# Local attention of a two-layer decoder: the rotation's second product in its own buffer, ahead of the sum of squares, and the sum's lower bound from a column in SBUF

## The chip, the core and the metric

The kernel runs on one core of a Trainium2 chip. A core has TensorE (PE in the profile, with its weight loads as PEld), VectorE (DVE), ScalarE (ACT), GpSimd (POOL) and SyncE (SP), which issues transfers. Each engine takes its instructions in the order of the program and waits on semaphores for the others. The metric is the device time of one execution in microseconds (us). It is the median of the runs.

## The reference, cut to what matters

The model is a decoder of two layers on x of 4 x 512 x 128. The change lies in the last block, a local attention with its feed-forward part, which has two layers of its own and runs over 4 x 512 tokens in each.

```
def l2norm(t):
    return t / jnp.clip(jnp.linalg.norm(t, axis=-1, keepdims=True), 1e-12)
def rotate_half(x):
    x1, x2 = jnp.split(x, 2, axis=-1)
    return jnp.concatenate([-x2, x1], axis=-1)
...
    h = shift_token(x)
    q, k, v = jnp.split(h @ wqkv, 3, axis=-1)      # 8 heads of 64
    q = l2norm(q) * qs
    k = l2norm(k) * ksc
    q = q * cos * scale + rotate_half(q) * sin * scale
    k = k * cos / scale + rotate_half(k) * sin / scale
    o = local_attention(q, k, v)                   # windows of 64, with the one before
    x = x + o @ wo
    h = layernorm(shift_token(x)) @ w1 + b1
    a, g = jnp.split(h, 2, axis=-1)
    x = x + (a * gelu(g)) @ w2 + b2
```

The norm's lower bound of 1e-12 becomes a bound of 1e-24 on the sum of squares.

## The kernel before, in words

The tokens are cut into 16 tiles of 128 (four for each of the four sequences). Two layers make 32 tiles, numbered `i` from 0 to 31. In the local attention nothing is scheduled by a planner: the order of every engine's queue is the order of the calls, written out by hand.

The main loop goes over `g`, two steps for each tile (`p` is 0 or 1, four of the eight heads each). A step calls `scores(g + 1)`, then `others(g, 0)`, `weights(g)`, `others(g, 1)`, `exponentials(g + 1)`, `values(g - 1)` and `others(g, 2)`. `others` takes its calls from the table `around` (L1805) with a distance in tiles: the projections of a tile start three tiles ahead of its attention. For tile `i + 3`:

- step p=0, slot 2: `project_qk` writes q and k of the tile into the PSUM buffer `pqk` (there is one), and `squares` (ScalarE) squares it into the SBUF buffer `sq` (there is one).
- step p=1, slot 0: `rotated_a` (VectorE) multiplies `pqk` by the cosine table into `ta`.
- step p=1, slot 1: `norms` (VectorE) sums `sq` over 64 into `ss` of 128x16 and bounds it from below (L1466, L1467). `rotated_b` follows: `halves` (VectorE, two instructions, L1480) multiplies the swapped halves of `pqk` by the sine table into `tb`. `halves_added` (POOL) adds `tb` to `ta`, `lengths` (POOL) raises `ss` to the power -0.5 into `rn`, and `scaled` (POOL) multiplies `ta` by `rn`.
- two tiles later `turn_k` and `turn_q` (PE) transpose the result into the PSUM buffers `ptk` and `ptq`.

`tb` has the tag `sq` with one buffer, so the square and the second product of a tile share one place in SBUF. `pqk` comes free when `sq`, `ta` and `tb` have been computed from it. It also serves the feed-forward part: `ff_gates`, in the step p=1, slot 2 of every fourth tile, puts its first two products `pff2` there.

PSUM tiles of the tag `pt` rotate over three buffers: `pv`, `po`, `ptp`, `ptk`, `ptq` and the feed-forward products take them in turn. A buffer comes free when it has been read: that of `po` by `xa` on VectorE (L1589), the residual sum in `output`, which stands behind `rotated_b` in the same step.

VectorE's order in the step with p=1 is: `nm` (the maximum of the scores, L1540), `ta`, `ss`, the bound, `tb`, then `rc` and `at` of `values` (L1570, L1571), then `xa`, then `nm` of the next step. In one step of every four tiles `ge` (L1641, a feed-forward product) stands between `tb` and `rc`.

Ahead of the main loop stands the cross attention, whose steps carry the first three tiles of the local attention in a list of their own, `first`. It calls `norms`, `rotated_a`, `halves`, `halves_added`, `lengths` and `scaled` one by one.

Of the kernel before, what the change touches and what calls it, by code (L numbers as in the profile page):

```python
# [11 lines left out]
F32 = mybir.dt.float32  # L12
# [3 lines left out]
ALU = mybir.AluOpType  # L16
# [3 lines left out]
P = 128  # L20
# [37 lines left out]
def decoder_kernel(ctx: ExitStack, tc: tile.TileContext, a: dict):  # L58
    nc = tc.nc
    V, S, G, TE = nc.vector, nc.scalar, nc.gpsimd, nc.tensor  # L60


    cp = ctx.enter_context(tc.tile_pool(name="const", bufs=1))
# [44 lines left out]
    G.memset(cminus, -1.0)  # L108
    eps = cp.tile([P, 1], F32, tag="eps", name="eps")
    G.memset(eps, 1e-5)  # L110


    hm16 = cp.tile([P, 16], F32, tag="hm16", name="hm16")
# [123 lines left out]
    with ExitStack() as ph:  # L237
# [176 lines left out]
        with tc.tile_pool(name="m2", bufs=3) as t2, \  # L414
# [159 lines left out]
            with tc.manual_schedule():  # L574
# [7 lines left out]
                for k in range(n_):  # L582
# [19 lines left out]
                    if aside and (n in (9, 10, 13, 14) or b == B - 1 and n < 11):  # L602
                        f, of = aside.pop(0)
# [815 lines left out]
    with tc.tile_pool(name="la_b", bufs=2) as bp, tc.tile_pool(name="la_t", bufs=2) as t1, \  # L1419
# [14 lines left out]
        hTs, pqks, tas, tbs, rns, sss, qTs, pes, pTs, ats, aTs = ({} for _ in range(11))  # L1434
# [28 lines left out]
        def norms(i):  # L1463

            ss = sm.tile([P, 16], F32, tag="ss16", name="ss16")
            V.tensor_reduce(ss, sss.pop(i).rearrange("p w h d -> p (w h) d"), AX.X, ALU.add)  # L1466
            V.tensor_scalar_max(ss, ss, 1e-24)  # L1467
            sss[i] = ss

        def rotated_a(i):  # L1470
# [3 lines left out]

        def halves(i):
            src = pqks.pop(i).rearrange("p w (h d) -> p w h d", d=64)
            tb = tbs[i] = t1.tile([P, 2, 8, 64], F32, tag="sq", name="tb", bufs=1)
            for hf in range(2):
                lo = slice(32 * hf, 32 * hf + 32)
                V.tensor_tensor(  # L1480
                    tb[:, :, :, lo], src[:, :, :, 32 - 32 * hf:64 - 32 * hf],
                    tabs[i // NT][:, i % NJ, 1, :, lo].unsqueeze(2).to_broadcast([P, 2, 8, 32]), ALU.mult)
# [11 lines left out]
            G.tensor_tensor(ta, ta, rns.pop(i).unsqueeze(2).to_broadcast([P, 16, 64]), ALU.mult)  # L1494

        def rotated_b(i):
            for f in (halves, halves_added, lengths, scaled):
                f(i)

        def turn_q(i):  # L1500
# [291 lines left out]
        def x_norm(b):  # L1792
            normal(x5[:, b * NJ:(b + 1) * NJ, :], *mvs.pop(("x", b)))


        first = {9: [(shift, 0)], 10: [(project_qk, 0), (squares, 0)],
                 11: [(norms, 0), (rotated_a, 0), (halves, 0), (halves_added, 0)],
                 12: [(project_qk, 1), (squares, 1), (lengths, 0)],
                 13: [(project_v, 0), (norms, 1), (rotated_a, 1), (halves, 1), (scaled, 0)],
                 14: [(halves_added, 1), (project_qk, 2), (squares, 2)], 15: [(lengths, 1), (turn_k, 0), (turn_q, 0)],  # L1800
                 16: [(project_v, 1), (norms, 2), (rotated_a, 2), (halves, 2), (scaled, 1)],
                 17: [(halves_added, 2)], 18: [(lengths, 2), (scores, 0)], 19: [(scaled, 2), (exponentials, 0)]}


        around = [[[], [(turn_k, 1), (turn_q, 1)], [(project_qk, 3), (squares, 3)]],  # L1805
                  [[(turn_out, -1), (rotated_a, 3)], [(norms, 3), (rotated_b, 3)], [(project_v, 2), (output, -1)]]]

        feed = {(0, 0): [[], [], [(ff_hidden, 2, 0)]], (0, 1): [[], [(ff_hidden, 2, 1)], []],
                (1, 0): [[(ff_shift, 1)], [(ff_hidden, 2, 2)], []],
# [14 lines left out]
        with tc.manual_schedule():  # L1824
# [25 lines left out]
            for g in range(last):  # L1850
                i, p = divmod(g, 2)
# [183 lines left out]
```

## Time and profile before

| | us |
|---|---|
| median of three runs | 1233.97 (1232.23 to 1235.54) |
| the profiled execution | 1233.73, its span 1231.7 |
| PE busy | 1081.4 (88%) |
| VectorE busy | 895.8 (73%) |
| ScalarE busy | 731.2 (59%) |
| POOL busy | 644.7 (52%) |
| `ss`, 32 sums | 38.7, 1209 ns each |
| the bound, 32 | 6.5, 202 ns each (174 in the median) |
| `tb`, 64 halves | 40.9, 681 ns each |
| POOL `ta<-ta,tb`, 32 | 75.4, 2356 ns each |
| POOL `rn`, 32 | 93.0, 2906 ns each |
| POOL `ta<-ta,rn`, 32 | 60.8, 1901 ns each |

The span is the time from the first to the last instruction on the core. Busy times of the engines overlap, and matmuls are pipelined, so a busy PE isn't a PE at its peak. In the rows, L1466 is line 1466 of the kernel; `out<-in` are the names of the tiles. The local attention's loop fills the trace from about 842 us to 1180 us, and the granted TensorE clock there is 1.00.

### The profile page before, as it was taken

What the parts mean: (1) busy time and instruction counts of PE and PEld (TensorE: products, weight loads), DVE (VectorE), ACT (ScalarE), POOL (GpSimd) and SP (SyncE); (2) the same over time, 40 slices, a digit from 0 to 9 for tenths busy, and PEclk for the clock granted to TensorE, in tenths of its full rate; (3) what the DMA queues carried; (4) which work ended last, traced back from release to release, by engine and by line L of the source; (5) the groups of instructions that cost most, each with busy time, mean ns of one, the idle gap of its engine ahead of it and who ended that gap; (6) DMA issues with size and microseconds to landing.
All of it is one profiled execution on the core that took longest, in us unless ns stands there. A gap on an engine that the chain in (4) does not pass through costs nothing.

```text
span 1231.7 us, 22149 instructions
## 1 busy us (share of the span) xinstructions
PE 1081.4 (88%) x8377; PEld 698.5 (57%) x8377; DVE 895.8 (73%) x1691; ACT 731.2 (59%) x1629; POOL 644.7 (52%) x554
## 2 busy tenths in 40 slices
PE   5879879787778889989999998787999999999995
PEld 2324333443456679966666665455666566666564
DVE  5878888898668274867867676787777676676753
ACT  5696867764364454546566665246665765766762
POOL 5458586776454432644201111367786576576641
PEclk9799989898799899999999999899999999999998
DMA  9000000000400342300000000000110110011100
GB/s 280 1 0 1 0 1 1 0 1 0 154 1 14 137 154 76 85 27 25 2 2 2 2 2 2 0 9 19 32 28 18 28 27 18 22 24 28 27 20 28
DMA packets 38739, 39.96 MB, mean 32 GB/s; under 512 B 7544, under 2 KB 29833, under 8 KB 38153
## 3 DMA queue, kind: packets, MB, share of 16 engines
q1 hardware_dynamic: 36041, 32.73, 9.2%
q0 software_dynamic: 2048, 4.20, 1.2%
q10 hardware_dynamic: 544, 1.62, 0.5%
q8 instruction: 66, 1.08, 0.4%
q14 instruction: 40, 0.33, 0.1%
HBM read 20.80 MB, written 9.18 MB: 24 GB/s over the span
## 4 chain that ended last, share of the span: by engine, by line
PE 46%; DVE 18%; ACT 4%; issue 2%; POOL 2%; DMA 1%; DVEq 0%; ACTq 0%; POOLq 0%; SPq 0%
PE psc L189 9%; PE pa L189 4%; PE pqk L189 4%; PE ptp L1287 4%; PE po L189 3%; PE pff L189 3%; PE phg L189 3%; PE pog L189 3%; DVE tb L1480 2%; PE pv L189 2%; DVE ss L1466 2%; DVE ta L1473 2%; PE pof L189 2%; PE pq L189 1%; DMA hn<-xa 1%
## 5 line engine op out<-in xcount | busy, mean ns | idle before, releaser
L451 POOL TENSOR_TENSOR h<-h,cb 128x1024 f32<-128x1024 f32 (+1 forms) x65 | 151.8, 2337 | 72.0 <-DVE h L446 59.8
L157 POOL TENSOR_TENSOR rs<-ve,cneg 128x1 f32<-128x1 f32 (+2 forms) x74 | 56.1, 758 | 210.9 <-DVE ve L166 175.7
L446 DVE TENSOR_TENSOR_SCAN h<-dA,pb 128x1024 f32<-128x1024 f32 x64 | 146.3, 2286 | 21.7 <-PE y L189 7.4
L1277 ACT ACTIVATE pe<-psc,nm 128x256 f32<-128x256 f32 (+1 forms) x256 | 93.4, 448 | 69.7 <-DVE nm L1270 68.9
L189 PE MATMUL y<-h,ident 128*128 128x512 f32 x256 | 128.9, 628 | 6.1 <-POOL h L451 5.4
L1486 POOL TENSOR_TENSOR ta<-ta,tb 128x1024 f32<-128x1024 f32 x32 | 75.4, 2356 | 102.5 <-DVE rc L1570 56.2
L1270 DVE TENSOR_REDUCE nm<-psc 128x4 f32<-128x1024 f32 (+1 forms) x64 | 69.8, 1090 | 43.1 <-PE psc L189 37.9
L157 POOL TENSOR_TENSOR rn<-ss,cneg 128x16 f32<-128x16 f32 x32 | 93.0, 2906 | 0.0
L1540 DVE TENSOR_REDUCE nm<-psc 128x4 f32<-128x512 f32 x64 | 44.0, 687 | 63.8 <-PE psc L189 62.0
L438 ACT ACTIVATE dA<-delta,negA 128x511 f32<-128x511 f32 (+1 forms) x128 | 85.3, 715 | 6.3 <-POOL delta L352 4.4
L189 PEld LDWEIGHTS y<-h,ident 128*128 128x128 f32 x256 | 49.7, 198 | 67.5 <-issue 47.2
L940 ACT ACTIVATE hTg<-phg,bias 128x128 f32<-128x128 f32 x184 | 52.3, 368 | 46.6 <-PE phg L189 45.0
L443 DVE TENSOR_TENSOR pb<-du,pb 128x1024 f32<-128x1024 f32 x64 | 77.5, 1211 | 2.4 <-POOL du L355 1.5
L1549 ACT ACTIVATE pe<-psc,nm 128x128 f32<-128x128 f32 x256 | 73.6, 380 | 5.0 <-DVE nm L1540 4.9
L189 PE MATMUL pqk<-f_qkv,hT 128*128 128x512 f32 x128 | 65.0, 631 | 4.1 <-DVE tb L1480 4.1
L1287 PE MATMUL ptp<-ident,pe 128*128 128x128 f32 x448 | 64.9, 282 | 4.0 <-ACT pT L1289 2.0
L189 PE MATMUL psc<-kb,qk 64*128 64x256 f32 (+1 forms) x512 | 66.4, 378 | 0.0
L189 PE MATMUL pb<-stk,sel 96*128 96x512 bf16 x128 | 41.2, 405 | 25.9 <-DVE h L446 15.5
L1494 POOL TENSOR_TENSOR ta<-ta,rn 128x1024 f32<-128x1024 f32 x32 | 60.8, 1901 | 2.4
L1287 PEld LDWEIGHTS ptp<-ident,pe 128*128 128x128 f32 x448 | 48.7, 141 | 20.4 <-ACT pT L1289 7.8
L1460 ACT ACTIVATE sq<-pqk 128x1024 f32<-128x1024 f32 x32 | 32.9, 1029 | 43.6 <-PE pqk L189 40.3
L189 PE MATMUL pff<-hnT,f_w 128*128 128x512 f32 (+3 forms) x108 | 48.7, 571 | 9.6 <-DVE tb L1480 7.3
(391 smaller groups left out, 2810.1 us busy)
## 6 DMA issues: line engine op xcount, KB each, us to landing
vh<-va SPq DMA_DIRECT2D x56, 130.0 KB
w<-in_e_w_dram SPq DMA_DIRECT2D x16, 256.0 KB
xs<-zero SPq DMA_DIRECT2D x2, 1472.0 KB
xg<-xs SPq DMA_DIRECT2D x10, 256.0 KB
ys<-yg SPq DMA_DIRECT2D x10, 256.0 KB
f_qkv<-in_f_qkv_dram SPq DMA_DIRECT2D x1, 1536.0 KB
x<-in_x_dram SPq DMA_DIRECT2D x4, 256.0 KB
w_kv<-in_w_kv_dram SPq DMA_DIRECT2D x1, 1024.0 KB
```

Source lines behind the costliest of these rows:

```text
L157: G.tensor_tensor(out, in_, cneg.to_broadcast([P, n]), ALU.pow)
L189: TE.matmul(out, lhsT=lhsT, rhs=rhs, start=start, stop=stop)
L438: S.activation(dAs[k % 4][:, c, c:T], delta[b % 2][:, c, c:T], AF.Exp, scale=negA[:, c * NST + n:c * NST + n + 1])
L443: V.tensor_tensor(pb, du[steps[k][0] % 2], pb, ALU.mult)
L446: V.tensor_tensor_scan(h.rearrange("p c t -> p (c t)"), dAs[k % 4].rearrange("p c t -> p (c t)"), pb.rearrange("p c t -> p (c t)"), 0.0, A ...
L451: G.tensor_tensor(h[:, c], h[:, c], cb.unsqueeze(1).to_broadcast([P, n, T]), ALU.mult)
L1270: V.tensor_reduce(nm, psc[:, :, 0:nk], AX.X, ALU.max, negate=True)
L1277: S.activation(pe[:, h, 0:nk], psc[:, h, 0:nk], AF.Exp, bias=nm[:, h:h + 1])
L1287: TE.transpose(ptp[:, h * nb + kk, :], pe[:, 2 * pr + h, kk * P:(kk + 1) * P], ident)
L1486: G.tensor_tensor(ta, ta, tbs.pop(i).rearrange("p w h d -> p (w h) d"), ALU.add)
L1494: G.tensor_tensor(ta, ta, rns.pop(i).unsqueeze(2).to_broadcast([P, 16, 64]), ALU.mult)
L1549: S.activation(pes[g][:, h, :], o[:, par, q, :], AF.Exp, bias=nm[:, k:k + 1])
```

## The change

Three edits. The product `tb` gets its own buffer, tag `tb`. In the main loop `norms` moves into `rotated_b`, behind `halves` and `halves_added` and ahead of `lengths`; in the lead-in list `first` the order stays. The bound is no longer a `tensor_scalar` with a number, but a `tensor_tensor` whose second input is a column `least` of SBUF, spread over 16 elements; POOL fills the column once at the start.

```diff
     eps = cp.tile([P, 1], F32, tag="eps", name="eps")
     G.memset(eps, 1e-5)
+    least = cp.tile([P, 1], F32, tag="least", name="least")
+    G.memset(least, 1e-24)
...
             V.tensor_reduce(ss, sss.pop(i).rearrange("p w h d -> p (w h) d"), AX.X, ALU.add)
-            V.tensor_scalar_max(ss, ss, 1e-24)
+            V.tensor_tensor(ss, ss, least.to_broadcast([P, 16]), ALU.max)
             sss[i] = ss
...
-            tb = tbs[i] = t1.tile([P, 2, 8, 64], F32, tag="sq", name="tb", bufs=1)
+            tb = tbs[i] = t1.tile([P, 2, 8, 64], F32, tag="tb", name="tb", bufs=1)
...
         def rotated_b(i):
-            for f in (halves, halves_added, lengths, scaled):
+            for f in (halves, halves_added, norms, lengths, scaled):
                 f(i)
...
-                  [[(turn_out, -1), (rotated_a, 3)], [(norms, 3), (rotated_b, 3)], [(project_v, 2), (output, -1)]]]
+                  [[(turn_out, -1), (rotated_a, 3)], [(rotated_b, 3)], [(project_v, 2), (output, -1)]]]
```

With it VectorE's order in the step with p=1 is `nm`, `ta`, `tb`, `ss`, the bound, `rc`, `at`, `xa`. POOL's order is the same as before, apart from the one `memset`. ScalarE's squares no longer wait for POOL; the queues of PE, ScalarE and SP keep their order.

## The prediction

> **What bounds the kernel now.** I began with the chain of work that ended last on the page.
>
> ```profile
> PE 46%; DVE 18%; ACT 4%; issue 2%; POOL 2%; DMA 1%; DVEq 0%; ACTq 0%; POOLq 0%; SPq 0%
> PE psc L189 9%; PE pa L189 4%; PE pqk L189 4%; PE ptp L1287 4%; PE po L189 3%; PE pff L189 3%; PE phg L189 3%; PE pog L189 3%; DVE tb L1480 2%; PE pv L189 2%; DVE ss L1466 2%; DVE ta L1473 2%; PE pof L189 2%; PE pq L189 1%; DMA hn<-xa 1%
> ```
>
> PE carries the chain, but three VectorE groups of the change's own stage stand in it: `tb`, `ss` and `ta`. That stage, the local attention, runs from 842 to 1180 us in the trace. The windows view has PE busy 45.6 of every 47.37 us there (a period of four token tiles), so it looks like a PE stage. The question is what releases PE. I read VectorE through one plain step in the timeline, then PE and POOL at the same place (columns: start us, us, engine, line, operation, out<-in).
>
> ```profile
> 942.97 1.21 DVE L1466 TENSOR_REDUCE ss<-sq 128x16 f32<-128x1024 f32 x1
> 944.21 0.17 DVE L1467 TENSOR_SCALAR ss<-ss 128x16 f32<-128x16 f32 x1
> 944.30 1.28 DVE L1480 TENSOR_TENSOR tb<-pqk,tab 128x512 f32<-128x512 f32 x2
> 945.49 0.17 DVE L1570 RECIPROCAL rc<-pa 128x4 f32<-128x4 f32 x1
> 945.70 0.42 DVE L1571 TENSOR_TENSOR at<-pa,rc 128x256 f32<-128x256 f32 x1
> 946.04 0.28 DVE L1589 TENSOR_TENSOR xa<-po,x 128x128 f32<-128x128 f32 x1
> ```
> ```profile
> 945.76 0.60 PE L1513 MATMUL ptk<-ident,ta 128*128 128x128 f32 x4
> 946.38 0.66 PE L1504 MATMUL ptq<-ident,ta 128*128 128x128 f32 x4
> ```
> ```profile
> 945.72 2.36 POOL L1486 TENSOR_TENSOR ta<-ta,tb 128x1024 f32<-128x1024 f32 x1 [2.65 <-DVE rc L1570]
> 948.04 2.90 POOL L157 TENSOR_TENSOR rn<-ss,cneg 128x16 f32<-128x16 f32 x1
> ```
>
> VectorE runs `ss`, its lower bound, `tb`, `rc`, `at`, `xa` without a hole. `xa` ends at 946.32 and `ptq`, which needs the PSUM buffer of `po` that `xa` reads, starts at 946.38. I compared `xa`'s end with `ptq`'s start in all 29 steps that hold `rotated_b` (tiles 3 to 31): in 21 of them `ptq` starts 0.06 to 0.09 us after `xa` ends, in tile 6 0.80 us after it, in tiles 10, 14, 18, 22, 26 and 30 3.7 to 4.6 us after it, and tile 3's step has no `xa`. So VectorE's queue and PE tie: PE hardly idles, but a VectorE queue that is longer at this place moves PE one for one. The only hole that PE itself shows in the stage is another one, in the waits of PE:
>
> ```profile
> PE pff L189 <- DVE tb L1480: 7.3, 6, 1.2
> ```
>
> These are the six tiles 10 to 30: the gate products `pff2` share the PSUM buffer of `pqk`, which `tb` is the last to read.
>
> **Part 1, `tb` in its own buffer and ahead of `ss`.** Let A be where `ss` starts today. `tb` then starts at A and not at A+1.33 (944.30-942.97), and ends at A+1.28. In the six gate steps `pff` waits 1.22 us, and `po` in front of it has ended when the wait starts, so 1.33 earlier clears it whole: 6 x 1.22 = **-7.3 us**. What comes next on PE there (`psc`, `pts`, `ptp`) has 3.7 us or more of room towards `xa`. The two waits of `pqk` for `tb` in the lead-in (2.31 and 1.74 us) stay: that list of steps calls `norms` ahead of `halves` as before.
>
> The own buffer also frees ScalarE's `sq` from POOL's sum. Today that wait ends last once, 3.3 us at 831.46. POOL itself runs without a hole from 828.07 to 842 there and VectorE idles only 1.17 and 0.19 us, so between 0 and 0.9 us come out; I take **-0.3**. The new `least` memset costs POOL what `eps` costs (0.10 us) ahead of a 0.78 us wait: nothing.
>
> **Part 2, the lower bound behind `tb`.** VectorE's work is the same: 1.28+1.21+0.17. What is new is the company. POOL's sum `ta<-ta,tb` starts 0.14 us after `tb` ends (945.72 against 945.58) and takes 2.36. Today VectorE is past the bound by then. Now POOL runs from A+1.42 to A+3.78, `ss` ends at A+2.40, and the bound is ready at A+2.43, in the middle of it. There is no row of a 128x16 `max` from two inputs. The nearest in kind and size is `ve<-mv,eps` (L179, 128x4, column of SBUF as second input), and it has two faces:
>
> ```profile
> 816.05 0.80 DVE L179 TENSOR_TENSOR ve<-mv,eps 128x4 f32<-128x4 f32 x1
> 948.56 0.16 DVE L179 TENSOR_TENSOR ve<-mv,eps 128x4 f32<-128x4 f32 x1
> ```
> ```profile
> 814.49 2.34 POOL L1486 TENSOR_TENSOR ta<-ta,tb 128x1024 f32<-128x1024 f32 x1 [2.65 <-DVE tb L1480]
> ```
>
> By the median row (0.162 us) the bound costs what it costs today, and the sum is -7.6. **The rule that speaks against the change** is in the Trainium skill, SBUF — State Buffer, section "Who interferes with whom": a VectorE instruction with two SBUF inputs shares a read port with GpSimd, and the one that comes second waits until the other has ended. By it the bound stays until A+3.78. The first `ve` above lies inside the very instruction in question and ends at 816.85, 0.02 us after POOL (816.83); two more at 159.41 and 229.44 last 2.02 and 2.01 us, to the end of POOL's scan product. The second `ve` lies in POOL's `rn` (948.04 to 950.94) and is not held, so the rule is wider than this trace: the power does not hold the port. The bound falls into the sum, not into the power, which needs its result. I take the block. The operand's form does not decide it: the old `tensor_scalar` was held once as well, 0.92 us at 898.79 behind POOL's `xab` add. At this place either form waits.
>
> So the bound ends at A+3.80, and `rc`, which starts 0.08 us before its predecessor's end (as `mx` did at 816.77), starts at A+3.72 instead of A+2.52 (945.49-942.97): **1.20 us later**. The bounds of this cost are 0 (not held) and 1.3 us.
>
> Behind it in VectorE's queue wait `rc`, `at`, `xa`, `nm`, and for `xa` waits `ptq` on PE:
> - 21 tied steps: 21 x 1.20 = +25.2. The steps whose `ge` stands between the bound and `rc` are among them; PE then stalls for the `pff` buffer first and for `xa` next, once together. No later step gives it back: VectorE's next idle (2.01 us before `nm`) is a wait for PE's `psc`.
> - Tile 6: 1.20 less its 0.80 of room: +0.4.
> - Tile 3: there `nm` holds the exponentials and these hold `psc` (1.07 us of PE wait at 857.61). `rc` +1.20, less the 0.11 that `ve` at 855.51 is held today by the same sum: +1.1.
> - The six gate steps: the 1.20 falls into 3.7 us and more: 0.
>
> POOL's `rn` and the scaling start 1.2 us earlier against VectorE; no PE wait in the stage names them, so nothing comes of it. But `ve` of the statistics, 0.52 us into `rn` today, slides 2.4 us against it, to its end (2.90): if the scaling (1.90 us) gets in first, VectorE loses up to 1.9 more, six times. VectorE idles 2.0 us before the next `nm` of those steps, which covers it; uncovered it is 11.4.
>
> **Sum:** -7.3 -0.3 +25.2 +0.4 +1.1 = +19.1. Against the profiled execution's 1233.73 (span 1231.7 and 2.0 around it) that is 1252.8; its time lies 0.24 below the median of the runs, 1233.97, so 1253.1. I say **1253**.
>
> **Rivals.**
> - *Not held* (10%): a 16-element instruction slips through as `ve` does at 948.56, and the change does what it promises: -7.6, 1226. Against it: that `ve` stood beside the power, and the three beside POOL sums or products of 1,024 columns were all held to the end. This is the other side; it decides if the bound's mean is under some 0.4 us.
> - *Held and more* (7%): the `ve` behind the scaling, or `ptq`, `qT`, exponentials late together, so that PE waits for ScalarE too: up to +19.1+11.4, 1264. It needs more than the 2.0 us of VectorE's idle.
> - *Cancelled* (3%): the block falls only where PE has room (gate steps), or in a third of the tied ones: 7 x 1.20 = 8.4 against 7.6, near 1234.
> - *The forecast* (80%): 1253, its own range 1244 to 1262 (1.0 us on 21 steps and all gains: +13; 1.3 us on 23 and no gain of `pff`: +30, which I cut a little).
>
> A difference of 0.3% (3.7 us) is what a measurement of this kernel can tell from none. Slower holds the forecast and the second rival, 0.87; same 0.03; faster 0.10. For 8 in 10 the range is 1243 to 1262.
>
> **What would show it.** The new bound at about 1.4 us in 29 rows, each ending 0.02 us after POOL's sum; `ss` still 1.21; `ptq` still right behind `xa` with some 1 us of PE wait for it; no PE wait of `pff` for `tb`; the four-tile period 47.4 - 1.2 + 3 x 1.2 = 49.8 us. Wrong if the bound stays at 0.17, or if `ptq` does not follow `xa`: then PE set the pace and the tie was chance.

## The result and the profile after

The changed kernel takes 1251.8 us (median, 1250.99 to 1255.18) against 1233.78 for the kernel before: a ratio of 1.0153, with an interval of 1.0139 to 1.0167. It is slower by 18 us in the medians and by 19 in the ratio. The forecast was 1253. The profiled execution has a span of 1250.2 us.

In the rows after the change all line numbers are larger by two. First the chain that ended last, on the page, by engine and by line:

```profile
PE 43%; DVE 22%; ACT 4%; issue 3%; POOL 2%; DMA 0%; DVEq 0%; ACTq 0%; POOLq 0%; SPq 0%
PE psc L191 9%; PE pqk L191 4%; PE pa L191 4%; PE ptp L1289 4%; PE po L191 3%; PE pff L191 3%; PE phg L191 3%; DVE ss L1469 3%; PE pog L191 3%; DVE tb L1482 2%; DVE ss L1468 2%; DVE ta L1475 2%; PE pof L191 2%; DVE nm L1542 1%; PE pq L191 1%
```

In the chain VectorE's share went from 18% to 22% of the span, and a name is new: `ss` of L1469, the bound of 16 elements, has 3% of the span, more than the sum of 1,024 that it follows. The view of its line (duration in ns: min/median/max) and the same plain step as before, VectorE, then POOL, then PE, in the timeline:

```profile
L1469 DVE TENSOR_TENSOR ss<-ss,least x32: 174/1370/1385, 810.2 to 1187.4; 128x16 f32<-128x16 f32 x32
```
```profile
949.48 1.28 DVE L1482 TENSOR_TENSOR tb<-pqk,tab 128x512 f32<-128x512 f32 x2
950.67 1.21 DVE L1468 TENSOR_REDUCE ss<-sq 128x16 f32<-128x1024 f32 x1
951.92 1.38 DVE L1469 TENSOR_TENSOR ss<-ss,least 128x16 f32<-128x16 f32 x1
953.22 0.17 DVE L1572 RECIPROCAL rc<-pa 128x4 f32<-128x4 f32 x1
...
953.76 0.28 DVE L1591 TENSOR_TENSOR xa<-po,x 128x128 f32<-128x128 f32 x1
```
```profile
950.90 2.36 POOL L1488 TENSOR_TENSOR ta<-ta,tb 128x1024 f32<-128x1024 f32 x1 [3.72 <-DVE tb L1482]
```
```profile
954.10 0.66 PE L1506 MATMUL ptq<-ident,ta 128*128 128x128 f32 x4 [1.23 <-DVE xa L1591]
```

The bound starts at 951.92, inside POOL's sum (950.90 to 953.26), and ends at 953.30. The sum of squares `ss`, which runs beside POOL's sum too, still takes 1.21. `xa` ends at 954.04, `ptq` starts at 954.10, and PE has now idled 1.23 us for it, where it idled 0.02 us before. The waits of PE in the stage (us in total, times, longest):

```profile
PE ptq L1506 <- DVE xa L1591: 18.3, 15, 1.2
PE ptk L1515 <- DVE rc L1572: 4.8, 6, 0.8
...
PE ptk L1515 <- DVE xa L1591: 1.3, 1, 1.3
```

The 7.3 us of `pff` for `tb` are gone from this list: what the edit was for has happened. In their place stand 24.4 us of waits for what is queued behind the bound: 15 times in front of `ptq`, once in front of `ptk` (tile 6), and 0.8 us each in front of `ptk` in the six steps where `ge` stands between the bound and `rc`.

To see where the time came from step by step I took the start of VectorE's `ta<-pqk,tab` of each of the 32 tiles and subtracted its start in the kernel before. A tied step is one in which PE starts right behind `xa` or behind something else in VectorE's queue; a gate step is one of the six (tiles 10, 14, 18, 22, 26 and 30) whose gate products use `pqk`; a plain step is a tied step without `ge`. From one tile to the next the difference grows by 1.17 to 1.22 us in 18 tied steps (in tile 31, the last, measured to its `ptq`), shrinks by 1.33 in each of the six gate steps (-8.0), and grows by 1.03, 0.96, 0.48, 1.13 and 1.15 in tiles 3, 6, 8, 24 and 28. From tile 3 to the `ptq` of tile 31 that is +18.4 us.

The difference of the spans is 18.5 (1250.2-1231.7), but it is not all from here. The first `ta` already starts 1.7 us earlier than before, the lead-in loses 1.0, and 0.7 come behind the last `ptq`; these happen to cancel. The traces of all the kernels below differ at the first `ta` by -3.8 to +1.5 us from the kernel before, though nothing but a `memset` or two was edited ahead of it. So the steps say more than a whole time.

### The profile page after: what moved, and what is told of

It is laid out like the page before. It is cut to its first block, busy times and chain, and to the rows that moved or that the text cites. A ratio compares the mean times of both kernels' runs of the same rounds, so it can differ in the third digit from the quotient of the medians.

```text
span 1250.2 us, 22150 instructions
## 1 busy us (share of the span) xinstructions
PE 1083.4 (87%) x8377; PEld 700.9 (56%) x8377; DVE 929.3 (74%) x1691; ACT 731.4 (59%) x1629; POOL 646.0 (52%) x555
## 4 chain that ended last, share of the span: by engine, by line
PE 43%; DVE 22%; ACT 4%; issue 3%; POOL 2%; DMA 0%; DVEq 0%; ACTq 0%; POOLq 0%; SPq 0%
PE psc L191 9%; PE pqk L191 4%; PE pa L191 4%; PE ptp L1289 4%; PE po L191 3%; PE pff L191 3%; PE phg L191 3%; DVE ss L1469 3%; PE pog L191 3%; DVE tb L1482 2%; DVE ss L1468 2%; DVE ta L1475 2%; PE pof L191 2%; DVE nm L1542 1%; PE pq L191 1%
## 5 line engine op out<-in xcount | busy, mean ns | idle before, releaser
L191 PE MATMUL phg<-xgT,wt 128*128 128x128 f32 x368 | 50.9, 282 | 4.7 <-DVE wt L934 4.5
```

Of the source, the lines that this page charges most:

```text
L191: TE.matmul(out, lhsT=lhsT, rhs=rhs, start=start, stop=stop)
```

## The experiments

**Is it the form of the bound, or its place?** The changed kernel with the old form:

```diff
-            V.tensor_tensor(ss, ss, least.to_broadcast([P, 16]), ALU.max)
+            V.tensor_scalar_max(ss, ss, 1e-24)
```

> The changed kernel with the old form of the bound, tensor_scalar with a number. Theory (the place behind tb puts the bound into POOL's sum, and either form is held there, as the old one was once for 0.92 us): the 29 bounds still last about 1.4 us and the time stays at 1252. Rival (the second SBUF input alone is what is held): the bounds last 0.17 us and the time falls to about 1226.

1251.65 us, ratio 1.0151 (1.0129 to 1.0174); here and below the ratio is to the kernel before, timed in the same session. The view of the line:

```profile
L1469 DVE TENSOR_SCALAR ss<-ss x32: 174/1370/1385, 809.3 to 1186.1; 128x16 f32<-128x16 f32 x32
```

With one SBUF input and a number it is held for the same 1.37 us. The form is not what costs. The reverse, the column form at the old place with the old buffers (the kernel before with `least` and the `tensor_tensor` line of the change):

> The kernel before with the bound from the column, order and buffers as before. Theory: the bound is past before POOL's sum starts, so 0.17 us each and 1234, within 0.3%. Rival (the column form costs by itself, wherever it stands): 1240 or more.

1234.66 us, ratio 1.0010 (0.9998 to 1.0023): no difference. The column costs nothing where no POOL sum runs beside it.

**The own buffer alone** (the kernel before, one edit):

```diff
-            tb = tbs[i] = t1.tile([P, 2, 8, 64], F32, tag="sq", name="tb", bufs=1)
+            tb = tbs[i] = t1.tile([P, 2, 8, 64], F32, tag="tb", name="tb", bufs=1)
```

> The kernel before with tb in its own buffer and nothing else. Theory: one ScalarE wait of 3.3 us goes, POOL and VectorE in the lead-in cover it: 1233 to 1234. Rival (the lead-in is paced by that wait): 1230.5.

1235.42 us, ratio 1.0011 (1.0001 to 1.0020). Neither expectation is met: it is not faster at all, and if anything 1 us slower. In its trace the starts of `ta` stand 0.8 us later than before from tile 3 on and stay there to the last tile. The first `ta` is 0.7 earlier, so the lead-in loses 1.5 us (the last section has it).

**Is the held bound the whole loss?** The changed kernel without it. The lower bound of the sums of squares is left out here.

```diff
             V.tensor_reduce(ss, sss.pop(i).rearrange("p w h d -> p (w h) d"), AX.X, ALU.add)
-            V.tensor_tensor(ss, ss, least.to_broadcast([P, 16]), ALU.max)
```

> The changed kernel without the bound (left out: the lower bound of the sums of squares). Theory (the held bound is the whole loss): rc starts 0.20 us earlier against ss than in the kernel before, the pff waits are gone: -7.3 for the gate steps, up to -3.6 for 21 tied steps with at most 0.17 of room on PE, 1222 to 1226. Rival (moving ss behind tb costs by itself, for instance through POOL's power): 1240 or more.

1219.86 us, ratio 0.9896 (0.9872 to 0.9921). So the order is right, and all of the loss is the one instruction: 1251.8 with it, 1219.9 without, for 29 instructions of 16 elements. It is 2 us better than expected. From tile to tile 0.1 to 0.2 comes out in most tied steps, 0.94 in tile 8, where the old bound had been held (see below), and 1.33 in gate steps.

**Does the tie of `xa` and `ptq` carry gains as well as losses?** The kernel before without the bound, the same line deleted in its old form and place; the lower bound is left out.

> The kernel before without the bound (left out: the lower bound of the sums of squares): VectorE's queue ahead of xa is 0.20 us shorter in each step. Theory (xa releases ptq, PE has some 0.17 us of room): 21 x 0.17 and 6 x 0.20 of the pff waits, -4.8, 1229. Rival (PE sets the pace, the tie of xa and ptq is chance): only the pff part, -1.2, 1232.6.

1231.79 us, ratio 0.9982 (0.9968 to 0.9997), nearer to the rival. But the experiment did not do what I meant it to:

```profile
940.59 1.21 DVE L1466 TENSOR_REDUCE ss<-sq 128x16 f32<-128x1024 f32 x1
941.91 1.29 DVE L1479 TENSOR_TENSOR tb<-pqk,tab 128x512 f32<-128x512 f32 x2
```

`tb` starts 1.32 us after `ss`, and it was 1.33 with the bound between them. In the shared buffer `tb` overwrites what `ss` reads, and starts only when `ss` has ended; the bound had filled that time. With its own buffer `tb` starts 1.14 us after `ss` in the same order (e11, below), 0.08 before `ss` ends. VectorE's queue did not get shorter here, so this run says nothing of the tie. It says that the bound was free at its old place in most steps of the main loop; only in tile 8 does its removal give 0.74 us, and in tiles 24 and 28 0.08 and 0.07.

**A longer queue with no port in it.** The kernel before with the sum of squares computed twice:

```diff
-            V.tensor_reduce(ss, sss.pop(i).rearrange("p w h d -> p (w h) d"), AX.X, ALU.add)
+            src = sss.pop(i).rearrange("p w h d -> p (w h) d")
+            V.tensor_reduce(ss, src, AX.X, ALU.add)
+            V.tensor_reduce(ss, src, AX.X, ALU.add)
```

> The kernel before with ss summed twice: VectorE's queue ahead of tb and xa is 1.13 us longer in each step, and no port is in question. Theory (a longer VectorE queue moves PE one for one): 21 x 1.13 in the tied steps, 0.3 and 1.1 in tiles 6 and 3, 6 x 1.13 at pff, 0 to 3 in the lead-in: +32 to +35, 1266 to 1269. Rival (PE sets the pace and the loss of the change is the lock's own): +7 to +10, 1241 to 1244.

1271.99 us, ratio 1.0316 (1.0290 to 1.0342): 39 us, far from the rival and 3 above the range of the theory. In the steps with `ge` and in the gate steps from tile 10 to 27 the difference grows by 1.25 or 1.26 a step (the second sum starts when the first has ended and adds 1.24 to VectorE's queue, not the 1.13 I took); in the lead-in it grows by 7.3, where I had allowed 3. In most plain steps it is only 0.47 to 0.87. There `ptq` no longer waits for `xa`; in some of them `pof`, the feed-forward's second product, does:

```profile
PE pff L189 <- DVE tb L1482: 14.8, 6, 2.5
PE ptq L1506 <- ACT pT L1559: 7.3, 20, 1.3
...
PE pof L189 <- DVE xa L1591: 1.6, 5, 0.3
```

That the three `pt` buffers have been dealt otherwise would explain it, but the trace does not name buffers. So the sum comes near by parts that do not agree, and the run supports the theory only in part: a longer VectorE queue moves PE one for one in the steps with `ge` and the gate steps, and by less where no `ptq` hangs on `xa`.

**The port, or any short instruction there?** The changed kernel with the bound as a maximum over two columns of one tile, 1e-24 standing in the second:

```diff
+        two = bp.tile([P, 16, 2], F32, tag="two", name="two", bufs=1)
+        V.memset(two, 1e-24)
...
-            V.tensor_reduce(ss, sss.pop(i).rearrange("p w h d -> p (w h) d"), AX.X, ALU.add)
-            V.tensor_tensor(ss, ss, least.to_broadcast([P, 16]), ALU.max)
+            V.tensor_reduce(two[:, :, 0:1], sss.pop(i).rearrange("p w h d -> p (w h) d"), AX.X, ALU.add)
+            V.tensor_reduce(ss, two, AX.X, ALU.max)
```

> The changed kernel with the bound as a tensor_reduce by max over two columns, one the sum and one 1e-24: one SBUF input, at the same place inside POOL's sum. Theory (the port, not the place as such): not held, about 0.2 us each, as ss itself runs beside POOL at 1.21: 1226. Rival (any short instruction there waits for POOL, for instance by a semaphore): about 1.4 us each and 1252.

1229.34 us, ratio 0.9955 (0.9937 to 0.9972). The line's view, one step of VectorE, and POOL beside it:

```profile
L1471 DVE TENSOR_REDUCE ss<-two x32: 185/186/187, 813.4 to 1166.6; 128x16 f32<-128x32 f32 x32
```
```profile
947.29 0.19 DVE L1471 TENSOR_REDUCE ss<-two 128x16 f32<-128x32 f32 x1
```
```profile
946.27 2.37 POOL L1490 TENSOR_TENSOR ta<-ta,tb 128x1024 f32<-128x1024 f32 x1 [2.67 <-DVE tb L1484]
```

Twice as many elements, the same result, the same place within POOL's sum, and 0.19 us instead of 1.37. What is held is a kind of access, not the place in the queue: a sum or maximum over one input passes. This form also writes to another tile than it reads, which the two held forms do not; but `ve<-mv,eps` in the prediction writes to another tile too and was held. The 3 us over the expected 1226 do not come from the bound: in the trace `ta` is 1.5 us late already at the first tile and 3.2 at tile 3. That execution was the slowest of five (1231.4), and the two fastest took 1226.3 and 1226.8.

**A held instruction with other work behind it.** The changed kernel with the column form moved behind `xa`, and the power and the scaling called after it. The first three tiles, in the lead-in, have no lower bound here.

```diff
-            for f in (halves, halves_added, norms, lengths, scaled):
+            for f in (halves, halves_added, norms):
...
+        def bound(i):
+            V.tensor_tensor(sss[i], sss[i], least.to_broadcast([P, 16]), ALU.max)
+            lengths(i)
+            scaled(i)
...
-                  [[(turn_out, -1), (rotated_a, 3)], [(rotated_b, 3)], [(project_v, 2), (output, -1)]]]
+                  [[(turn_out, -1), (rotated_a, 3)], [(rotated_b, 3)], [(project_v, 2), (output, -1), (bound, 3)]]]
```

> The changed kernel with the bound (column form) moved behind xa in VectorE's queue, the power and the scaling after it (left out: the bound of the first three tiles, in the lead-in). Theory (a held instruction costs what waits behind it): the bound is ready about 0.7 us before POOL's sum ends, so it is held that long, but in front of nm and not of xa; nm has that much room, and the time is within 3 us of the kernel without a bound, 1219 to 1224. Rival (any wait in VectorE's queue reaches PE): 29 x 0.6 more, 1235 to 1240.

1222.65 us, ratio 0.9924 (0.9902 to 0.9945). One step of VectorE, then POOL:

```profile
942.67 0.28 DVE L1595 TENSOR_TENSOR xa<-po,x 128x128 f32<-128x128 f32 x1
942.87 0.75 DVE L1502 TENSOR_TENSOR ss<-ss,least 128x16 f32<-128x16 f32 x1
943.55 0.68 DVE L1546 TENSOR_REDUCE nm<-psc 128x4 f32<-128x512 f32 x1
```
```profile
941.23 2.37 POOL L1487 TENSOR_TENSOR ta<-ta,tb 128x1024 f32<-128x1024 f32 x1 [2.23 <-DVE tb L1481]
```

It is still held (0.75 us, to 943.62, POOL's sum ends at 943.60), in 23 of 29 steps for 0.73 to 0.88 us; in the six with `ge` POOL's sum is nearly over and it takes 0.16 or 0.17. It costs next to nothing: `nm` behind it has that much room, `xa` ahead of it is on time. From tile to tile it goes as e4 does, but for 0.8 us more in tiles 3 and 8 and 0.5 in tile 29.

**The version that beats both kernels.** With its own buffer the square can have a 65th column that holds 1e-24 for good. The sum over 65 then cannot be below it, and the bound as an instruction is gone. (The column is added to every sum, where the reference takes the larger of the two; that differs only for sums that are themselves as tiny.) Against the changed kernel:

```diff
+        sq65 = bp.tile([P, 2, 8, 65], F32, tag="sq65", name="sq65", bufs=1)
+        V.memset(sq65[:, :, :, 64:65], 1e-24)
...
-            sq = t1.tile([P, 2, 8, 64], F32, tag="sq", name="sq", bufs=1)
-            S.activation(sq, pqks[i].rearrange("p w (h d) -> p w h d", d=64), AF.Square)
-            sss[i] = sq
+            S.activation(sq65[:, :, :, 0:64], pqks[i].rearrange("p w (h d) -> p w h d", d=64), AF.Square)
+            sss[i] = sq65
...
-            V.tensor_tensor(ss, ss, least.to_broadcast([P, 16]), ALU.max)
```

> The changed kernel with the bound's instruction gone and its job done in the sum: the squares get a 65th column that holds 1e-24 once and for all, so that the sum can't be below it. Theory: no instruction is left for POOL's sum to hold, ss 0.02 us longer: 1222 to 1226, the fastest. Rival (ss itself is held once it takes longer or POOL runs beside it): 1240 or more.

1220.45 us, ratio 0.9890 (0.9872 to 0.9909): 1.1% under the kernel before, with the floor kept. And the same kernel with `ss` ahead of `tb` again (`norms` back in its own place in `around`):

> The kernel with the floor in the sum (65th column, no bound instruction) and its own buffer for tb, but ss ahead of tb as in the kernel before. Theory (two gains apart: the order clears the pff waits, the own buffer with no bound lets tb follow ss 0.2 us sooner, which reaches PE through xa): the pff waits of six times 1.0 us stay, 21 x 0.2 is kept, so 6 to 8 us over the same kernel with tb first (1220.5), 1227 to 1229. Rival (the order is worth nothing once the bound is gone): 1220 to 1222.

1229.98 us, ratio 0.9965 (0.9947 to 0.9982), 1 us above the range of the theory. PE waits for `tb` again, six times 1.0 us:

```profile
PE pff L191 <- DVE tb L1482: 6.2, 6, 1.0
```

From tile to tile the plain steps keep their 0.19 us and the gate steps change by 0.19 instead of 1.3. So the order is worth 1.14 us in each of six gate steps, 6.8 together, as soon as nothing in it is held. The medians of the two kernels differ by 9.5; the other 2.7 us I could not place.

## Why the prediction was right, point by point

- **The bound is held by POOL's sum.** Forecast: ready at A+2.43, ended at A+3.80, `rc` 1.20 later. In the step shown A is 949.48: ready at A+2.44, ended at A+3.82, `rc` at A+3.74 (A+2.52 before). Each of the 29 ends 0.03 or 0.04 us after POOL's sum. The rule of the Trainium skill (SBUF — State Buffer, "Who interferes with whom") and the long row of `ve` had it; the median row would have given 1226. That the form does not decide is shown by e1, that the access does by e7.
- **`xa` sets `ptq`.** Forecast: 21 steps at 1.20. Measured: 18 steps at 1.17 to 1.22. In the six with `ge` PE stands for 0.8 us in front of `ptk` and hardly longer in front of `ptq`: once together, as forecast. The period of four tiles is 49.7 us, forecast 49.8. That a gain passes as well shows in e4 (0.1 to 0.2 a step), not in e5, which did not shorten the queue.
- **Mis-sized steps.** Tile 6 got +0.4 and cost 0.96. I had taken the distance from `xa` to `ptq` for room, but in that step it is `ptk` that takes the buffer of `po`; it starts right behind `xa` and now waits 1.28 us for it. Tile 8 got 1.20 and cost 0.48: there the old bound had been held 0.92 us already, the very row that I quoted, and I did not subtract it:

```profile
898.79 0.92 DVE L1467 TENSOR_SCALAR ss<-ss 128x16 f32<-128x16 f32 x1
```
```profile
898.41 1.26 POOL L1601 TENSOR_TENSOR xab<-xa,row 128x512 f32<-128x512 f32 x1
```

  Tiles 24 and 28 likewise, by 0.07 and 0.05. The two errors, +0.56 and -0.72, cancel by luck.
- **The gate steps.** Forecast -7.3, measured 6 x 1.33 = -8.0, and e11 shows that it is the order that gives it.
- **`ve` of the statistics.** It did slide to the end of the power and slipped in ahead of the scaling: 0.16 us in all six steps, as in the first of the two cases named. It was a near thing: `ve` started only 0.07 to 0.09 us before the scaling did.
- **The lead-in.** Forecast -0.3; from the first `ta` to that of tile 3 the changed kernel loses 1.0 us and e3, the buffer alone, 1.5. The step that failed is that clearing ScalarE's wait could only gain. It was small beside the rest.
- **The sum.** From tile 3 on 26.7-7.3 = +19.4 was forecast and +18.4 measured. One sum of the prediction does not come out: the low end of its own range, 1244, does not follow from the +13 beside it, which gives 1247.

## What to carry to other kernels

Before an instruction is moved, look at what the neighbouring engine runs at its new place, not only at what it waits for: 16 elements took 1.37 us because an independent addition on POOL ran beside them. Judge a short instruction by its longest rows and by what ran then, not by the median. And where such an instruction must stay, give it another access (a reduction, a constant column within a sum that is computed anyway) or put it behind the instruction that others wait for.

## What the runs showed of the hardware that I had not expected

The own buffer lets ScalarE go on early in the lead-in: its wait of 3.3 us for POOL's sum is gone in every kernel with that buffer. PE's work there moves with it. PE's long hole, 3.38 us ending at 833.62 in the kernel before, becomes one of 2.75 us that ends at 836.25 for POOL's `xpr`. Behind it the granted TensorE clock falls to 0.50, although the longer hole of the kernel before left it at 1.00.

The traces show where the two differ. In each of the twelve the granted clock changes only at times that lie a whole number of 3.413 us apart; in the changed kernel 837.00 and 840.41 are two of them. So I cut the time into stretches of that grid. The windows view (stretch, us, busy of PE, PEld, DVE, ACT and POOL with counts, granted TensorE clock, DMA) of the changed kernel, then of the kernel before, then of e2, which has the order and the hole (3.38 us, ending at 832.01) of the kernel before:

```profile
833.59:837.00 3.41, 0.66 (x4) 0.42 (x4) 2.48 (x4) 1.77 (x5) 3.25 (x6) 1.00 0.23 52
837.00:840.41 3.41, 3.01 (x28) 2.66 (x28) 0.29 (x1) 0.82 (x2) 3.41 (x3) 0.50 0.02 5
```
```profile
828.24:831.65 3.41, 2.00 (x16) 1.76 (x16) 3.23 (x9) 0.19 (x1) 3.41 (x3) 1.00 0.01 2
831.65:835.07 3.42, 1.45 (x13) 1.48 (x14) 2.00 (x8) 2.90 (x5) 3.42 (x2) 1.00 0.00 0
```
```profile
829.89:833.31 3.42, 1.30 (x12) 1.33 (x13) 2.14 (x9) 3.04 (x5) 3.42 (x2) 1.00 0.00 0
```

In the changed kernel nearly the whole hole lies in one stretch, PE is busy there for 0.66 us of 3.41, and the next stretch has half the clock. In the kernel before the longer hole is split over two stretches with 2.00 and 1.45 us busy, and neither is followed by a drop. In e2 the same hole lies a little differently on the grid, one stretch has 1.30, and the clock behind it, from 833.31 to 836.72, is 0.50. In all eight kernels with an own buffer the stretch of the hole has PE busy for 19% or 20%, and the clock drops. Over the twelve traces each of the 145 full-clock stretches with PE busy below 42% was followed by half the clock; of the busier ones some were, most not, so the busy share is not the whole rule.

A group of eight `pox` products takes 2.08 us at the lower clock against 1.06 to 1.16 in the kernel before. From the first `ta` to that of tile 3 the kernels with an own buffer lose 0.8 to 2.4 us against the kernel before, those without it -0.4 to +0.2 (e8, which adds work there, aside). e2 is among the latter in spite of its stretch at half the clock, so the clock alone does not make the loss; what part of it is the clock's stays open.
